# Gate rows made in four column strips of the array and spread to all partitions by DMA through device memory

## The chip, the cores and the metric

The kernel runs on one core of a Trainium2 chip. The core has a matrix engine (TensorE, called PE in the profile, with its weight loads as PEld), a vector engine (VectorE, DVE), a scalar engine (ScalarE, ACT), a general engine (GpSimd, POOL) and a synchronisation engine (SyncE, SP). Each runs its own instructions strictly in order and waits on semaphores for the others. The metric is the device time of one execution in microseconds; lower is better. Before the change the median of three runs is 1042.11 us (1041.72 to 1042.24).

## The reference, cut to what matters

Two transformer layers run over x of shape (4, 1024, 256), in float32. The first layer modulates its three branches by nine vectors made from a condition vector per batch entry; three of the nine are gates that multiply what a branch adds to x:

```python
m = silu(mod) @ w_ada + b_ada                      # (4, 9*256)
sh_msa, sc_msa, g_msa, sh_mca, sc_mca, g_mca, sh_mlp, sc_mlp, g_mlp = split(m, 9)
x = x + self_attn(ln(x) * (1 + sc_msa) + sh_msa) * g_msa       # ends in  o @ w_so + b_so
x = x + topk_cross_attn(ln(x) * (1 + sc_mca) + sh_mca) * g_mca # ends in  o @ w_co + b_co
x = x + swiglu(ln(x) * (1 + sc_mlp) + sh_mlp) * g_mlp          # ends in  h @ w_m2 + b_m2
```

The second layer is a cross-attention without gates. Self-attention works in windows of 128 tokens, and the cross-attention of the first layer keeps the 16 largest scores of 77 for each head and token.

## The kernel before

The 4 x 1024 tokens are cut into 16 units of 256 tokens, four to a batch entry b. Each unit passes five stages: windowed self-attention, selection of the top 16 scores, the cross-attention with them, the MLP, and the attention of the second layer. All units are written down as operations of a planner (`Plan`, lines 222 to 379): an operation has an engine, a cost, a function that issues its instructions, the buffers that it reads and writes, and a priority. `place` puts the operations in an order by these costs and priorities, and `issue` calls the functions in the order of their planned starts. So the order of instructions on each engine is fixed when the program is built, and the planned costs set it, not the measured ones. Where the plan has a gap on PE, `issue` fills it with small matmuls (line 1335) on a bank that is free.

A gate multiplies a whole output row, so the kernel multiplies it into the weight columns and the bias row instead: w_so, w_co and w_m2 (and b_so, b_co, b_m2) are loaded anew for each b and multiplied on POOL by the gate of that b. This takes two steps.

First, once, in `mod_gate(i)` (lines 721 to 731) for each of the three gates: PE multiplies the four silu'd condition vectors, held as columns in `sc_t`, by a chunk of w_ada (line 727), which gives 4 rows of 256 in a bank of the accumulator memory (PSUM), and DVE adds the bias row and stores them in `gates`, 4 partitions of 3 x 256 (line 730). `sc_t` is padded with zeros to 32 columns. The neighbour `mod_group` (line 699) works differently: it splits its chunk into four parts of 128 columns, and each part is multiplied in its own strip of 32 columns of the array, so that part j lands on partitions 32j to 32j+31.

Second, in `gated(b)` (lines 1292 to 1314), twelve times (b = 0 to 3, three gates): the row of b must stand on all 128 partitions. PE does this with a matmul whose stationary operand is one column of the identity, broadcast to 128 columns (line 1303); ACT copies the result from the bank to an SBUF buffer `gate` (line 1306; there are two such buffers); and POOL multiplies first the bias row (line 1308) and then the weights (line 1310) by it. The multiply of the weights waits for their load, and the load for the last reader of the buffer's old contents, so it can come much later than that of the row.

Other lines that the text below speaks of: 592, every load of weights, rows and biases, issued from SP (but for two bias loads at the start, which ACT issues); 699 and 706, strips and transpose of the other modulations; 748 and 755, transposes and modulation of the second layer's context; 767, 771, 780 and 783, keys and values of the context; 902, 905, 907, 909 and 912, a layer norm: statistics on DVE, the power -1/2 on POOL, subtract and multiply on DVE; 919, its transpose on PE; 926, the modulation on ACT; 938 and 1075, projections; 961 to 973, the shift that makes exponentials safe (POOL, PE, ACT); 985 and 996, scores and their maxima; 1098 and 1104, scores again with the shift, into the one buffer `s`; 1108, the exponential; 1116, times the values; 1008 to 1025, the division by the sum (ACT, POOL, DVE); 1035 and 1044, the output projection and its addition to x; 1049, the addition of the gated bias row to x on POOL; 1145 to 1166, the top-16 selection on DVE; 1247 and 1275, the MLP.

Of the kernel before, what the change touches and what calls it, by code (L numbers as in the profile page):

```python
# [9 lines left out]
F32 = mybir.dt.float32  # L10
BF16 = mybir.dt.bfloat16
AF = mybir.ActivationFunctionType
ALU = mybir.AluOpType
# [3 lines left out]
P = 128  # L17
# [371 lines left out]
def tile_block(ctx: ExitStack, tc: tile.TileContext, a: dict, out: bass.AP):  # L389
    nc = tc.nc  # L390

    x_d, cond_d, ctx_d = a["x"], a["cond_1024"], a["ctx_1024"]
    B, L, C = x_d.shape
# [3 lines left out]
    KC = C // P  # L397
# [12 lines left out]
    def ctile(shape, name, dt=F32):  # L410
        return const.tile(shape, dt, tag=name, name=name)
# [7 lines left out]
    ident = ctile([P, P], "ident")  # L419
# [25 lines left out]
    for i in range(3):  # L445
        t = ctile([P, TU, 4, 32], f"parts{i}", BF16)
# [5 lines left out]
    for i in range(2):  # L452
        t = ctile([P, TU, H // 2, VP], f"v_self{i}")
# [3 lines left out]
    pl = Plan()  # L457


    def f_pe(cols, n):  # L460
        return n * (cols * 0.00175 + 0.0095) + 0.1

    def f_act(n):
        return 0.21 + 0.00081 * n

    def f_dve(n):
        return 0.155 + 0.00104 * n

    def f_pool(n):
        return 0.13 + 0.00222 * n  # L470
# [7 lines left out]
    T_GATE = ("D", "D", 0.22, 0.05, 0.37, 0.216)  # L478
# [7 lines left out]
    def f_dma(kb):  # L486
        return max(0.4, kb / 260.0)


    def fixed(name, shape, dt=F32):  # L490
        return pl.fixed(ctile(shape, name, dt), name)
# [7 lines left out]
    bp = fixed("bp", [P, C])  # L499
    n_mod = 26  # L500
    mod = fixed("mod", [P, n_mod, B])
    gates = fixed("gates", [B, 3, C])
    k_ctx = [fixed(f"k_{i}", [P, KC, B, 2, LC]) for i in range(2)]
    v_ctx = [fixed(f"v_{i}", [LC, B, H // 2, VP]) for i in range(2)]
    for v, fill in zip(v_ctx, (0.0, 1.0)):
# [7 lines left out]
    start, total = {}, 0  # L513
# [6 lines left out]
    class Place:  # L520
# [21 lines left out]
        def buf(self, name, shape):  # L542
            ap, lo = self.ap(shape)
            b = pl.fixed(ap, name)
            early.append((lo, self.at, b))
            return b
# [12 lines left out]
    at = Place(0)  # L559
# [3 lines left out]

    sc_t = at.buf("sc_t", [P, KC, 32])
    nc.gpsimd.memset(sc_t(), 0.0)
    bg_ada = at.buf("bg_ada", [B, 3, C])
    cx = at.buf("cx", [LC, B, C])
    cn = at.buf("cn", [LC, B, C])
    w_kv = [at.buf("w_kv0", [P, KC, 2 * C])]
# [3 lines left out]
    at = Place(start["slab"])  # L573
# [15 lines left out]
    def load(buf, src, kb, prio, key=None, eng="SP", view=None):  # L589
        def fn():  # L590
            dst = buf() if view is None else view(buf())
            (nc.sync if eng == "SP" else nc.scalar).dma_start(dst, src)
        pl.op(eng, f_dma(kb) if eng == "SP" else 0.3, fn, w=[buf if key is None else (buf, key)],
              prio=prio, lag=2.0)
# [8 lines left out]
    def row_bc(buf, name, lo, prio, key=None, view=None, np_=P):  # L603
        load(buf, a[name][lo : lo + C].partition_broadcast(np_), np_, prio, key, view=view)
# [11 lines left out]
    for g, names in enumerate(groups):  # L616
        for name, hi in names:
            n, r = hi // P, n_rows[g]
# [2 lines left out]
            col_of[name] = (g, r)  # L621
            n_rows[g] += n
    for i in range(3):
        row_bc(bg_ada, "L0_xcond_b_ada", (3 * i + 2) * C, (-79.5, -59.5, -49.5)[i], i, lambda t, i=i: t[:, i, :], B)
    row_bc(bv_self, "L0_xcond_b_qkv", 2 * C, -81)
    row_bc(bv_ctx[0], "L0_xcond_b_kv", C, -66)
    row_bc(bv_ctx[1], "L1_xcond_bkv", C, -29.5)
# [2 lines left out]
    def chunk(name, lo, n, prio):  # L630
        c = pl.buf("chunk", f"{name}{lo}")
        load(c, a[name].rearrange("(kc p) n -> p kc n", p=P)[:, :, lo : lo + n], n, prio,
             view=lambda t: t[:, :, :n])
        early.append((chunk_lo, chunk_hi, c))
        return c
# [85 lines left out]
    def mod_gate(i, prio, dma_prio):  # L721
        c = chunk("L0_xcond_w_ada", (3 * i + 2) * C, C, dma_prio)
        pp = pl.buf("mm", f"modg{i}")

        def fn():
            for kc in range(KC):
                nc.tensor.matmul(pp()[:B, :C], sc_t()[:, kc, :B], c()[:, kc, :C],
                                 start=(kc == 0), stop=(kc == KC - 1))
        pl.op("PE", f_pe(C, 2), fn, w=[pp], r=[sc_t, c], prio=prio)
        pl.op("DVE", f_dve(256), lambda: nc.vector.tensor_tensor(  # L730
            gates()[:, i, :], pp()[:B, :C], bg_ada()[:, i, :], ALU.add), w=[(gates, i)], r=[pp, (bg_ada, i)], prio=prio)

    def filled(v):

# [55 lines left out]
    for i, key in enumerate("kqv"):  # L790
        weight(w_qkv, "L0_xcond_w_qkv", -84 + i, (1, 0, 2)[i] * C, C, key)
    mod_gate(0, -30, -79)
    mod_group("L0_xcond_w_ada", 3 * C, 6, False, -3, -70)
    load(cx, ctx_d.rearrange("b k c -> k b c"), 308, -69)
    weight(w_kv[0], "L0_xcond_w_kv", -68)
    weight(w_q0, "L0_xcond_w_q", -67)
    mod_gate(1, -2, -59)
    mod_group("L0_xcond_w_ada", 6 * C, 12, False, -1, -50)
    mod_gate(2, -1, -49)
    mod_group("L1_xcond_Wss_q", 0, 18, True, -1, -48)  # L800
    mod_group("L1_xcond_Wss_kv", 0, 22, True, -1, -47)
    for q in range(4):
        lo = (q % 2) * HID + (q // 2) * 4 * P
# [7 lines left out]
    for b in range(B):  # L811
        pl.op("DVE", 0.42, lambda b=b: nc.vector.bn_stats(st_c()[:LC, b, :], cx()[:, b, :]),
              w=[(st_c, b)], r=[cx], prio=-1)
    for b in range(B):
        pl.op("DVE", 0.16, lambda b=b: nc.vector.bn_aggr(mv_c()[:LC, b, :], st_c()[:LC, b, :]),
              w=[(mv_c, b)], r=[(st_c, b)], prio=-1)
# [475 lines left out]
    def gated(b, pr):  # L1292

        gw = {}
        for i, (key, name, kc) in enumerate(
            (("so", "L0_xcond_w_so", KC), ("co", "L0_xcond_w_co", KC), ("m2", "L0_xcond_w_m2", NF))
        ):
            first = None if b else DMA_FIRST[i]
            w, row = pl.buf("w_" + key, f"w_{key}{b}"), pl.buf("row", f"b_{key}{b}")
            gate, pg = pl.buf("gate", f"gate{b}{i}"), pl.buf("mm", f"pg{b}{i}")  # L1300
            load(w, a[name].rearrange("(kc p) n -> p kc n", p=P), 128 * kc, first or pr)
            load(row, a[f"L0_xcond_b_{key}"].partition_broadcast(P), 128, first or pr)
            pl.op("PE:gate", T_GATE, lambda i=i, pg=pg: nc.tensor.matmul(
                pg()[:, :C], ident[:B, b : b + 1].to_broadcast([B, P]), gates()[:, i, :], start=True, stop=True),
                w=[pg], r=[(gates, i)], prio=pr, take=[gate])
            pl.op("ACT:gate", f_act(256), lambda gate=gate, pg=pg: nc.scalar.copy(gate(), pg()[:, :C]),
                  w=[gate], r=[pg], prio=pr)
            pl.op("POOL:gate", f_pool(256), lambda row=row, gate=gate: nc.gpsimd.tensor_tensor(
                row(), row(), gate(), ALU.mult), w=[row], r=[row, gate], prio=pr)
            pl.op("POOL:gate", f_pool(256 * kc), lambda w=w, gate=gate, kc=kc: nc.gpsimd.tensor_tensor(  # L1310
                w(), w(), gate().unsqueeze(1).to_broadcast([P, kc, C]), ALU.mult),
                w=[w], r=[w, gate], prio=pr)
            gw["b_" + key], gw["w_" + key] = row, w
        return gw

    stages = (self_attention, selection, cross_attention, mlp, last_attention)
    for b in range(B):
        pl.at = None
        gw = gated(b, b * NU - 0.5)
        for part in range(NU):  # L1320
            u = Unit()
            u.b, u.part, u.name = b, part, f"_{b}{part}"
            u.prio = float(b * NU + part)
            pl.at = None
            u.x = pl.buf("x", "x" + u.name)
            move_x(u, x_d, False)
            for k, stage in enumerate(stages):
                pl.at = (b * NU + part, k)
                u.prio = ORDER[b * NU + part][k]
                stage(u, gw)  # L1330
# [45 lines left out]
```

## Time and profile before

| what | value |
|---|---|
| median of 3 runs | 1042.11 us |
| the profiled execution, its own time | 1041.43 us |
| its span, first to last instruction | 1039.4 us |
| mean granted TensorE clock | 0.993 |
| DVE, ACT and POOL busy | 73%, 70%, 52% of the span |
| line 1303, spread of the gates: PE | 24 records, 9.6 us busy |
| line 1306, copy of the gates: ACT | 12 instructions, 386 ns in the mean |
| line 1308, row times gate: POOL | 12 instructions, 724 ns; 33.9 us idle before them |
| line 1310, weights times gate: POOL | 12 instructions, 1.27 us for 512 columns, 4.53 us for 2048 |
| line 727, making the gates: PE | 12 records, 3.1 us busy |
| line 730, bias of the gates: DVE | 3 instructions, 412 ns |

A line of a timeline holds the start in us, the busy time in us, the engine, the line of the kernel, the operation, what it writes and reads with shapes, how many instructions of that kind were merged, and in brackets how long the engine was idle before it and what released it. One float32 matmul shows as two records. A granted clock of 1.00 is TensorE's full speed.

### The profile page before, as it was taken

The numbers are of one execution on the slowest core, as the hardware profiler recorded it, in microseconds if no ns is written. First come the engines' busy times: TensorE is split into PE (matmuls) and PEld (weight loads), VectorE is DVE, ScalarE is ACT, GpSimd is POOL, SyncE is SP. The second block draws the span as 40 slices with busy tenths as digits, with TensorE's granted clock in tenths as the row PEclk, the third lists the DMA queues.
The fourth block names the chain that finished last, engine by engine and source line by source line (L and its number), as shares of the span: only waits on it lengthen the run. The fifth ranks groups of instructions, "written<-read, shape, count | busy, mean of one in ns | idle before, by whom it ended". The sixth has DMA issues, their size and how long they took to land.

```text
span 1039.4 us, 27476 instructions
## 1 busy us (share of the span) xinstructions
PE 1012.0 (97%) x10363; PEld 770.5 (74%) x10363; DVE 757.3 (73%) x4000; ACT 723.5 (70%) x1270; POOL 542.1 (52%) x751
## 2 busy tenths in 40 slices
PE   7899999999999999999999999999999999999997
PEld 5667777777777778777877777778767787778775
DVE  5177999979899999947833446599999977724232
ACT  3358786687687794758468667877688765764665
POOL 3384445466353573557635647546335464753653
PEclk9799999999999999999999999999999999999999
DMA  7710000001000000100000200000000001000000
GB/s 255 242 50 7 3 2 1 3 3 36 3 22 27 7 3 5 38 16 22 21 1 2 82 22 21 2 2 2 2 2 22 2 2 42 12 1 12 2 21 21
DMA packets 23623, 27.01 MB, mean 26 GB/s; under 512 B 1609, under 2 KB 20675, under 8 KB 23491
## 3 DMA queue, kind: packets, MB, share of 16 engines
q1 hardware_dynamic: 23455, 25.26, 7.7%
q8 instruction: 81, 1.33, 0.5%
q14 instruction: 52, 0.42, 0.1%
q10 hardware_dynamic: 35, 0.01, 0.0%
HBM read 21.07 MB, written 4.19 MB: 24 GB/s over the span
## 4 chain that ended last, share of the span: by engine, by line
PE 48%; DVE 13%; ACT 6%; POOL 2%; issue 1%; POOLq 0%; ACTq 0%; DVEq 0%
PE mm L1247 13%; PE mm L1275 8%; PE mm L938 5%; PE mm L1035 5%; PE s L1196 4%; PE o L1212 3%; PE s L985 3%; DVE share L1153 2%; DVE r L1147 2%; DVE nm L996 2%; PE s L1186 1%; DVE share L1145 1%; DVE share L1151 1%; PE mm L919 1%; ACT prob L1108 1%
## 5 line engine op out<-in xcount | busy, mean ns | idle before, releaser
L1247 PE MATMUL mm<-share,w_m 128*128 128x256 f32 x640 | 150.3, 386 | 0.4 <-ACT share L926 0.2
L1205 ACT ACTIVATE prob<-s 77x2048 f32<-77x2048 f32 x64 | 120.0, 1875 | 43.7 <-PE s L1201 43.4
L996 DVE TENSOR_REDUCE nm<-s 128x16 f32<-128x2048 f32 (+1 forms) x64 | 119.0, 1859 | 38.0 <-PE s L985 17.2
L1247 PEld LDWEIGHTS mm<-share,w_m 128*128 128x128 f32 x640 | 117.7, 190 | 26.0 <-issue 4.7
L1147 DVE MATCH_REPLACE8 r<-share 128x77 f32<-128x77 f32 x512 | 109.9, 222 | 0.0
L1145 DVE MAX8 share<-share 128x8 f32<-128x77 f32 x512 | 94.4, 225 | 21.0 <-ACT share L1138 21.0
L1153 DVE MATCH_REPLACE8 share<-share,r 128x77 f32<-128x77 f32 x512 | 109.6, 221 | 0.0
L1011 POOL TENSOR_TENSOR share<-share 128x256 f32<-128x256 f32 x64 | 47.1, 736 | 96.4 <-ACT share L1008 95.1
L1151 DVE MAX8 share<-r 128x8 f32<-128x77 f32 x512 | 93.9, 224 | 0.0
L1247 PE MATMUL mm<-slab,w_m 128*128 128x256 f32 x384 | 92.9, 388 | 0.7 <-ACT slab L926 0.5
L1023 POOL TENSOR_TENSOR slab<-slab,share 128x256 f32<-128x256 f32 x96 | 69.4, 730 | 28.4 <-ACT share L1018 19.2
L1261 POOL TENSOR_SCALAR slab<-slab 128x512 f32<-128x512 f32 x43 | 64.4, 1498 | 36.8 <-ACT slab L1259 33.0
L1247 PEld LDWEIGHTS mm<-slab,w_m 128*128 128x128 f32 x384 | 69.9, 190 | 15.6 <-issue 3.1
L1275 PE MATMUL mm<-share,slab 128*128 128x256 f32 x344 | 80.9, 381 | 0.0
L1008 ACT ACTIVATE share<-o,mask 128x256 f32<-128x256 f32 x128 | 66.6, 575 | 12.2 <-PE o L1212 9.6
L1108 ACT ACTIVATE prob<-s 128x2048 f32<-128x2048 f32 x32 | 60.5, 1889 | 17.9 <-PE s L1104 17.5
L1044 DVE TENSOR_TENSOR slab<-slab,mm 128x512 f32<-128x512 f32 x52 | 35.4, 680 | 50.9 <-PE mm L1035 25.7
L1275 PEld LDWEIGHTS mm<-share,slab 128*128 128x128 f32 x344 | 64.7, 190 | 10.0 <-issue 0.9
L1253 ACT ACTIVATE slab<-mm,cols 128x256 f32<-128x256 f32 x90 | 43.0, 480 | 41.0 <-PE mm L1247 40.5
L1212 PE MATMUL o<-prob,v 77*32 77x256 f32 x1024 | 67.9, 385 | 0.8 <-ACT share L1018 0.5
L1049 POOL TENSOR_TENSOR slab<-slab,row 128x512 f32<-128x512 f32 x39 | 49.9, 1278 | 28.5 <-DVE slab L912 15.4
L907 POOL TENSOR_SCALAR rs<-mv 128x2 f32<-128x2 f32 x64 | 14.2, 222 | 81.7 <-DVE mv L905 78.8
(183 smaller groups left out, 2427.0 us busy)
## 6 DMA issues: line engine op xcount, KB each, us to landing
share<-in_L_xcond_w_m_dram SPq DMA_DIRECT2D x4, 1024.0 KB
slab<-in_x_dram SPq DMA_DIRECT2D x9, 256.0 KB, 2.9
out_dram<-slab SPq DMA_DIRECT2D x9, 256.0 KB, 2.7
w_m<-in_L_xcond_w_m_dram SPq DMA_DIRECT2D x4, 512.0 KB, 6.8
share<-in_L_xcond_w_ada_dram SPq DMA_DIRECT2D x3, 512.0 KB, 3.8
w_so<-in_L_xcond_w_so_dram SPq DMA_DIRECT2D x4, 256.0 KB
w_co<-in_L_xcond_w_co_dram SPq DMA_DIRECT2D x4, 256.0 KB, 4.0
w_qkv<-in_L_xcond_w_qkv_dram SPq DMA_DIRECT2D x3, 256.0 KB
```

What stands on the lines that cost most here:

```text
L996: pl.op("DVE:max", f_dve(n), lambda: nc.vector.tensor_reduce(nm()[:, t], s4(), AX.X, ALU.max, negate=True), w=[(nm, t)], r=[s], prio=u.prio)
L1008: pl.op("ACT:nln", 0.5, lambda e=e, own=own, other=other: nc.scalar.activation(nz()[:, e, :], o()[:, ts(e, UT)], AF.Ln, bias=own, scale=ot ...
L1023: nc.gpsimd.tensor_tensor(dst, dst, shaped(nz()[:, k, :], dst), op)
L1108: pl.op("ACT:exp", f_act(2048), lambda s=s, prob=prob: nc.scalar.activation(prob(), s(), AF.Exp), w=[prob], r=[s], prio=pr)
L1145: nc.vector.max(top()[:, h + i, 0:8], sc()[:, h + i])
L1147: nc.vector.match_replace(r1()[:, i], top()[:, h + i, 0:8], sc()[:, h + i], NEG)
L1151: nc.vector.max(top()[:, h + i, 8:16], r1()[:, i])
L1153: nc.vector.match_replace(sc()[:, h + i], top()[:, h + i, 8:16], r1()[:, i], NEG)
L1205: pl.op("ACT:exp", f_act(2048), lambda s=s, prob=prob: nc.scalar.activation(prob()[:LC], s()[:LC], AF.Exp), w=[prob], r=[s], prio=pr)
L1212: nc.tensor.matmul(o()[r, :UT] if drops is not None else o()[r, ts(e, UT)], columns(v_z()[:, b], 8 * c + 2 * j + e), prob()[:LC, j, ts(e, ...
L1247: nc.tensor.matmul(pp()[:, ts(half, UT)], w_m1()[:, kc, m : m + P], ht()[:, kc, :], start=(kc == 0), stop=(kc == KC - 1))
L1275: nc.tensor.matmul(pp()[:, ts(t, C)], gts[f // 2]()[:, f % 2, ts(t, P)], w_m2()[:, f, :], start=(f == 0), stop=(f == NF - 1))
```

## The change

The gates are made in four strips of the array, as the other modulations are: for each half of the contraction four matmuls of 64 columns take the place of one of 256. The row of gate i and batch entry b then lies in four pieces of 64 numbers on partitions b, 32+b, 64+b and 96+b. DVE's addition works on 128 partitions of 64, and the bias that it adds is loaded as 128 runs of 64 numbers instead of 4 of 256. Right after that addition POOL issues a DMA that writes the 128 x 64 block to device memory. In `gated`, the operation of PE issues no matmul any more: it issues, on POOL's queue, a DMA that reads the four pieces back from device memory into all 128 partitions of `gate`. ACT's copy issues nothing. Both operations stay in the plan with their old engines and costs, so the planned order is the same; only what they issue differs. The kernel before issues no DMA from POOL at all; the changed one issues three writes of 32 KB and twelve reads of 128 KB there.

```diff
-    gates = fixed("gates", [B, 3, C])
+    gates = fixed("gates", [P, 3, C // 4])
+    dram = ctx.enter_context(tc.tile_pool(name="dram", bufs=1, space=bass.MemoryType.DRAM))
+    gates_d = [dram.tile([P, C // 4], F32, tag=f"gates_d{i}", name=f"gates_d{i}") for i in range(3)]
...
-    bg_ada = at.buf("bg_ada", [B, 3, C])
+    bg_ada = at.buf("bg_ada", [P, 3, C // 4])
...
     for i in range(3):
-        row_bc(bg_ada, "L0_xcond_b_ada", (3 * i + 2) * C, (-79.5, -59.5, -49.5)[i], i, lambda t, i=i: t[:, i, :], B)
+        lo = (3 * i + 2) * C
+        load(bg_ada, a["L0_xcond_b_ada"][lo : lo + C].rearrange("(j o n) -> j o n", j=4, o=1).to_broadcast([4, 32, C // 4]),
+             B, (-79.5, -59.5, -49.5)[i], i, view=lambda t, i=i: t[:, i, :])
...
             for kc in range(KC):
-                nc.tensor.matmul(pp()[:B, :C], sc_t()[:, kc, :B], c()[:, kc, :C],
-                                 start=(kc == 0), stop=(kc == KC - 1))
+                for j in range(4):
+                    nc.tensor.matmul(pp()[32 * j : 32 * j + 32, : C // 4], sc_t()[:, kc, :], c()[:, kc, ts(j, C // 4)],
+                                     start=(kc == 0), stop=(kc == KC - 1))
         pl.op("PE", f_pe(C, 2), fn, w=[pp], r=[sc_t, c], prio=prio)
-        pl.op("DVE", f_dve(256), lambda: nc.vector.tensor_tensor(
-            gates()[:, i, :], pp()[:B, :C], bg_ada()[:, i, :], ALU.add), w=[(gates, i)], r=[pp, (bg_ada, i)], prio=prio)
+        def add():
+            nc.vector.tensor_tensor(gates()[:, i, :], pp()[:, : C // 4], bg_ada()[:, i, :], ALU.add)
+            nc.gpsimd.dma_start(gates_d[i], gates()[:, i, :])
+        pl.op("DVE", f_dve(256), add, w=[(gates, i)], r=[pp, (bg_ada, i)], prio=prio)
...
-            pl.op("PE:gate", T_GATE, lambda i=i, pg=pg: nc.tensor.matmul(
-                pg()[:, :C], ident[:B, b : b + 1].to_broadcast([B, P]), gates()[:, i, :], start=True, stop=True),
+            pl.op("PE:gate", T_GATE, lambda i=i, gate=gate: nc.gpsimd.dma_start(
+                gate().rearrange("p (j n) -> p j n", j=4),
+                gates_d[i].rearrange("(j r) n -> r j n", j=4)[b].partition_broadcast(P)),
                 w=[pg], r=[(gates, i)], prio=pr, take=[gate])
-            pl.op("ACT:gate", f_act(256), lambda gate=gate, pg=pg: nc.scalar.copy(gate(), pg()[:, :C]),
-                  w=[gate], r=[pg], prio=pr)
+            pl.op("ACT:gate", f_act(256), lambda: None, w=[gate], r=[pg], prio=pr)
```

## The prediction

> **What bounds the kernel.** I read the page's busy shares and slices first:
>
> ```profile
> PE 1012.0 (97%) x10363; PEld 770.5 (74%) x10363; DVE 757.3 (73%) x4000; ACT 723.5 (70%) x1270; POOL 542.1 (52%) x751
> ...
> DVE  5177999979899999947833446599999977724232
> ...
> PEclk9799999999999999999999999999999999999999
> DMA  7710000001000000100000200000000001000000
> ```
>
> PE is full, but DVE is nearly full in slices 4 to 16 (104 to 442 us, with dips at 7 and 8), and slice 1 (26 to 52 us) has DMA traffic and a low clock; by windows of 1 us it is 0.50 from 36 to 48 us. The chain of waits could be followed back only to 309.8 us; of those 730 us PE has 68%, DVE 19%.
>
> Next, who waits for the spreading matmuls (the view of line 1303; idle columns are us, times):
>
> ```profile
> L1303 PE MATMUL mm<-gates,ident x24: 372/454/791, 34.5 to 563.7; 4*128 4x256 f32 x24
> ...
> who waited for it (us, times):
>   ACT gate L1306: 7.4, 4
> ```
>
> Then POOL's timeline, since all new work lands on its queue:
>
> ```profile
> 35.63 0.72 POOL L1308 TENSOR_TENSOR row<-row,gate 128x256 f32<-128x256 f32 x1 [11.50 <-DMA w_m<-in_L_xcond_w_m_dram]
> 36.32 1.26 POOL L1310 TENSOR_TENSOR w_so<-w_so,gate 128x512 f32<-128x512 f32 x1
> 38.98 0.72 POOL L1308 TENSOR_TENSOR row<-row,gate 128x256 f32<-128x256 f32 x1 [1.41 <-ACT gate L1306]
> 39.66 1.27 POOL L1310 TENSOR_TENSOR w_co<-w_co,gate 128x512 f32<-128x512 f32 x1
> ...
> 46.80 0.72 POOL L1308 TENSOR_TENSOR row<-row,gate 128x256 f32<-128x256 f32 x1
> 52.09 0.73 POOL L1011 TENSOR_TENSOR share<-share 128x256 f32<-128x256 f32 x1 [4.56 <-ACT share L1008]
> ```
>
> The first batch of gates ends at 47.5 and leaves POOL 4.56 us of slack. Later gates have less:
>
> ```profile
> 118.71 0.73 POOL L1308 TENSOR_TENSOR row<-row,gate 128x256 f32<-128x256 f32 x1 [2.59 <-ACT gate L1306]
> 119.40 1.28 POOL L1049 TENSOR_TENSOR slab<-slab,row 128x512 f32<-128x512 f32 x1
> 120.76 0.22 POOL L907 TENSOR_SCALAR rs<-mv 128x2 f32<-128x2 f32 x1
> 121.07 0.71 POOL L909 TENSOR_TENSOR rs<-rs,mhalf 128x2 f32<-128x2 f32 x1
> ```
>
> That rs, done at 121.78, is used by DVE's L912 at 121.91, with DVE full: 0.13 us of slack.
>
> **What goes.** Twelve spreading matmuls at about 0.62 us a pair (0.59 to 0.69 in PE's timeline where nothing is interleaved): 7.4 us of PE. Worth on the path: at 527.88 the pair is on the chain, -0.6. At 89.93 PE is full (19.95 of 20 us between 80 and 100), -0.6. At 103.66, 117.53, 336.08 and 507.29 DVE is full or the chain, at 271.32 filler follows, at 563.40 the chain is on ACT: 0. The four between 34 and 43 us run at half clock; without them the second L1098 (46.91) could start 1.6 us sooner, but the division it leads to (POOL L1011) is behind POOL, see below: 0. Twelve ACT copies of 0.37: none on the chain, 0. Making the gates: line 699 does 512 columns in strips in 0.65 us, so 256 take at least 0.33, against 0.96 now; at most -0.6 three times, but PE waits at 33.12 for a load anyway: 0. DVE's addition of 64 columns: 0.2 shorter, 0. The bias loads of 128 runs cost SP 0.47 instead of 0.28 (the row of bv_self): +0.2, under SP's later wait of 8.9 us for PE; without that cover +0.6. Sum: **-1.2**.
>
> **What comes.** No DMA issued by POOL is in this trace. Each read is 512 runs of 256 B. Holding POOL: at least 0.4 (SP issues a row load in 0.34 to 0.47 us). POOL's own slope is (4.53-1.27)/1536 = 2.1 ns an element; one such step a run is 0.2+1.1 = 1.3 us, two (read and write side in turn) 2.4. I take 1.3. Then landing: quiet, x loads of 256 KB take 2.9 us from issue; 128 KB row loads, nearest in size and broadcast, all took longer:
>
> ```profile
> DMA to landing us min/median/max: 4.6/5.6/6.7
> ```
>
> Less SP's issue of 0.4 that is 2.5 quiet and 5.2 beside the weight loads (DMA share about 0.9 from 31 to 50 us). So a read lands 3.8 us after its start when quiet, 6.5 early.
>
> *Early batch.* Queue order on POOL: write of gate 2 (after DVE at 31.2, done 31.7), read 0, row, w_so, read 1, read 2 (same buffer as read 0, so behind w_so), row, w_co, L1049, a read for b=1, w_m2, row, L1011. Read 0 starts at 31.7, lands 38.2; row and w_so to 40.2; reads 1 and 2 hold POOL to 42.8; read 1 lands 46.7; row, w_co, L1049 to 49.9; the next read to 51.2; w_m2 (4.5) and row to 56.5. L1011 is **4.4 us late** (52.09). Behind it stand the rs at 52.90, then DVE L912 (54.91) and PE's transpose at 56.04. POOL's gap of 1.44 before 55.36 takes up part; after it there is none until 66.9 us, and DVE's L912 at 63.50 waits for that queue: **+3.0**.
>
> *Gate 0 of b=2.* Read issued at 116.12, lands 119.9, not 118.71: 1.2 late, less 0.13: **+1.1** on a full DVE.
>
> *The rest.* Issued ahead into idle stretches of 6.26, 4.14 and 8.49 us that now end at ACT's copy or a maximum (107.77, 272.54, 530.88): hidden; with no stretch each would cost 1.3. At 94.67 read at 91.7, 0.8 late, taken by the gap of 1.78 before 100.09. At 337.25 1.8 late, but PE needs the parts at 341.67, 1.6 after they were made, and 0.96 of gap lies between. At 508.37 2.2 late, gap of 4.02 behind it. At 573.49 the read starts eight multiplies ahead. All 0.
>
> Sum: -1.2+3.0+1.1 = **+2.9**: 1041.43 becomes 1044.3; runs had a median 0.7 above that execution, so **1045.0**.
>
> **Rules weighed.** The Trainium skill (DMA: Bandwidth & Descriptors, Anatomy of one DMA) gives 2.0 us plus bytes/436e3 for a DMA from POOL: an estimate of 2.3 us for 128 KB, against my row's 5.2. With it a read lands 3.6 after issue, the early batch ends at 50.6, before 52.09, and the sum is -1.2+0.9 = -0.3: 1041.8. I stay with the row: same size, same broadcast, same stretch. Against the change speaks SBUF — State Buffer, SBUF: two separate sides: POOL cannot write descriptors while DVE holds the port both share, 0.62 us becoming 3.1 in its example. The trace shows such sharing: L912 twice at 508.90 takes 1.69 us beside POOL's L1310, 0.72 at 121.91. By the rule the read at 116.12 would be 2.5 later, sum +5.4; but the DVE work beside it then is a maximum (L996), of another kind, so I add nothing and keep this for the range.
>
> **Rivals.**
> 1. *Faster.* PE bounds all of it and POOL's waits are hidden: POOL loses 22.4 us of waiting for ACT's copies. 7.4 us times PE's share of 68% is -5.0: **1037**. It decides if reads land within 3.6 us and the early batch ends by 52. Against it: DVE is near full from 104 to 442 us.
> 2. *No change.* The rule's 2.3 us holds, gains and the late b=2 gate cancel: **1041.8**.
> 3. *Much slower.* POOL is held 2.4 us a read and reads land at the worst row's 6.3 behind that. The early batch then ends at 62.3, 10.2 late, +8.8; b=2 +2.2; at 337 +0.4; less 1.2: +10.2, **1052**. It decides if one read holds POOL over 2 us. Less work on PE in 28 to 43 us could also keep it at half clock longer, in the same direction.
>
> **Numbers.** Forecast 0.52 (own range 1043 to 1048), rival 1 0.17, rival 2 0.16, rival 3 0.15. A difference under 0.2% (2.1 us) is not told from none: of the forecast 0.10 falls inside. Faster 0.17; same 0.16+0.10 = 0.26; slower 0.42+0.15 = 0.57. The range 1038.5 to 1052 leaves out the better half of rival 1 and the worse half of rival 3.
>
> **What would show it.** In the changed profile: POOL's L1011 for unit 0 near 56 instead of 52 (rival 3: over 60; rivals 1 and 2: at 52 or before); POOL's issue of a read near 1.3 us; DVE idle about 1 us before L912 near 122; clock windows of 0.50 still ending near 48; POOL waiting for its own reads in place of ACT. I am wrong if POOL catches up before 52 us, or if the early lateness, visible at 60 us, is gone by 104 us where DVE fills.

## The result, and the profile after

| | before | after |
|---|---|---|
| time, median (range) | 1041.91 us (1041.71 to 1042.24, 4 runs) | 1071.16 us (1070.21 to 1073.40, 4 runs) |
| ratio | | 1.0283, 95% interval 1.0266 to 1.0301 |
| the profiled execution, its span | 1041.43, 1039.4 us | 1070.21, 1068.4 us |

The changed kernel is slower by 29 us. The sign was forecast, the size was not: +2.9 was expected, and the range ended at 1052.

The busy times of the changed kernel and its DMA row (40 slices of the span):

```profile
PE 1010.2 (95%) x10375; PEld 770.8 (72%) x10375; DVE 756.3 (71%) x4000; ACT 720.8 (67%) x1258; POOL 553.8 (52%) x766
...
DMA  7951300000100200100120311000000001000000
```

Every engine has nearly the same work as before, so 29 us are waiting. The DMA row shows where to look first: slices 1 to 3 are 9, 5 and 1 in place of 7, 1 and 0. The part on DMA queues has a column for the share of 16 engines' time:

```profile
q1 hardware_dynamic: 23827, 25.34, 7.7%
q0 software_dynamic: 672, 1.67, 4.5%
```

Queue 0 holds the writes and reads of the gates. It moves 1.67 MB and takes more than half as much engine time as the 25.34 MB of all other loads and stores. The view of the reads' line, with durations in ns and landing in us, and then of POOL's wait:

```profile
L1314 POOL DMA_DIRECT2D gate<-gates_d x12: 747/841/866, 30.7 to 592.1; - x12
...
who waited for it (us, times):
  POOL row L1319: 50.6, 8
...
DMA to landing us min/median/max: 4.9/8.3/13.5
```

One read holds POOL for 0.84 us, less than the 1.3 assumed. It lands after 8.3 us in the median; 3.8 (quiet) and 6.5 (early) were assumed.

**Where the time comes from.** DVE runs the same 4000 instructions in the same order in both kernels, so the start of each can be compared with that of its counterpart. The difference, called the shift below, is a staircase: -0.2 us at 20 us of the old time, up and down from 30 to 55 (between -4 and +12), about +10 from 56 to 100, +11 to 119, +19 from 127, +18 at 330, +25 from 351, +29 from 521, and it stays there to the end. So four places make the loss: one near 50 us (10 us) and three later ones (8, 7 and 3.4 us). The later ones look alike in POOL's timeline, where brackets hold the idle time and what ended it. At the first:

```profile
126.97 0.84 POOL L1314 DMA_DIRECT2D gate<-gates_d  x1
135.49 0.71 POOL L1319 TENSOR_TENSOR row<-row,gate 128x256 f32<-128x256 f32 x1 [7.68 <-DMA gate<-gates_d]
136.17 1.25 POOL L1059 TENSOR_TENSOR slab<-slab,row 128x512 f32<-128x512 f32 x1
137.51 0.22 POOL L917 TENSOR_SCALAR rs<-mv 128x2 f32<-128x2 f32 x1
137.81 0.73 POOL L919 TENSOR_TENSOR rs<-rs,mhalf 128x2 f32<-128x2 f32 x1
```

and DVE's timeline beside it:

```profile
138.57 0.73 DVE L922 TENSOR_SCALAR share<-slab,mv,rs 128x256 f32<-128x256 f32 x2 [5.63 <-POOL rs L919]
```

POOL stands 7.68 us for its own read. Behind that read are an addition and the rs that DVE needs: DVE, full in this stretch before, idles 5.63 us. The read issued at 353.67 lands at 362.03, with the parts for TensorE behind it; the one issued at 532.20 lands at 540.51.

The early place looks different. A window of 6 us, first in the kernel before, then in the changed one; behind the window and its length stand busy us and counts of PE, PEld, DVE, ACT and POOL, the granted clock, the DMA share (of 16 engines) and GB/s:

```profile
48.00:54.00 6.00, 6.00 (x111) 4.49 (x108) 1.80 (x8) 4.78 (x8) 1.67 (x3) 0.94 0.81 211
48.00:54.00 6.00, 6.00 (x48) 3.84 (x46) 0.00 (x0) 4.03 (x9) 3.47 (x4) 0.72 1.22 43
```

From 48 to 54 us the DMA engines show a share of 1.22 and move 43 GB/s; before the change it was 0.81 and 211 GB/s. (The view counts the whole time of a packet in the window where the packet starts, so a share can pass 1.) The queues of this window in the changed kernel, with packets, MB and share:

```profile
q0 software_dynamic: 54, 0.16, 114.6%
q1 hardware_dynamic: 104, 0.10, 7.3%
```

So nearly all of that time belongs to the gates' reads, and hardly anything else moves. SP's own timeline shows who suffers; the kernel before, then the changed one, for the five x loads of that stage (from the start of the first to the end of the last, SP's waits for earlier loads between them included):

```profile
39.60 6.53 SPq L892 DMA_DIRECT2D slab<-in_x_dram  x5
```

```profile
42.90 12.05 SPq L902 DMA_DIRECT2D slab<-in_x_dram  x5
```

Both POOL and DVE then start late:

```profile
57.55 4.50 POOL L1321 TENSOR_TENSOR share<-share,gate 128x2048 f32<-128x2048 f32 x1 [3.11 <-issue]
59.73 0.75 DVE L912 BATCH_NORM_STATS2 st<-slab 128x6 f32<-128x256 f32 x2 [15.44 <-DMA slab<-in_x_dram]
```

The view names no releaser for POOL, but the third read, issued at 43.89, lands after 13.5 us, at 57.4. So at 50 us there are two candidates, POOL's wait for the reads and the loads held up behind them, and the page alone does not tell which one counts. The clock is not a third: in the changed kernel it is 0.50 again from 60 to 68 us, but the shift does not grow over that stretch (11.6 us for the DVE instruction at 59.73, 10.9 for the one at 70.87).

### The profile page after: what moved, and what is told of

Read it like the earlier page. It is cut to its first block, busy times and chain, and to the rows that moved or that the text cites. A ratio compares the mean times of both kernels' runs of the same rounds, so it can differ in the third digit from the quotient of the medians.

```text
span 1068.4 us, 27505 instructions
## 1 busy us (share of the span) xinstructions
PE 1010.2 (95%) x10375; PEld 770.8 (72%) x10375; DVE 756.3 (71%) x4000; ACT 720.8 (67%) x1258; POOL 553.8 (52%) x766
## 3 DMA queue, kind: packets, MB, share of 16 engines
q1 hardware_dynamic: 23827, 25.34, 7.7%
q0 software_dynamic: 672, 1.67, 4.5%
## 4 chain that ended last, share of the span: by engine, by line
PE 60%; DVE 17%; ACT 8%; POOL 5%; DMA 4%; issue 3%; POOLq 0%; ACTq 0%; DVEq 0%
PE mm L1257 15%; PE mm L1285 8%; PE mm L948 7%; PE mm L1045 6%; PE s L995 5%; PE s L1206 5%; PE o L1222 4%; DVE r L1157 3%; DVE share L1163 3%; DVE nm L1006 2%; PE s L1196 2%; DVE share L1155 2%; DVE share L1161 2%; PE mm L929 2%; PE s L1108 2%
## 5 line engine op out<-in xcount | busy, mean ns | idle before, releaser
L1215 ACT ACTIVATE prob<-s 77x2048 f32<-77x2048 f32 x64 | 120.0, 1875 | 46.1 <-PE s L1211 45.7
L1006 DVE TENSOR_REDUCE nm<-s 128x16 f32<-128x2048 f32 (+1 forms) x64 | 119.0, 1859 | 39.8 <-PE s L995 19.3
L1021 POOL TENSOR_TENSOR share<-share 128x256 f32<-128x256 f32 x64 | 46.9, 732 | 87.7 <-ACT share L1018 83.2
L1118 ACT ACTIVATE prob<-s 128x2048 f32<-128x2048 f32 x32 | 60.3, 1885 | 16.7 <-PE s L1114 16.3
```

The lines of the kernel that those rows point to most:

```text
L1006: pl.op("DVE:max", f_dve(n), lambda: nc.vector.tensor_reduce(nm()[:, t], s4(), AX.X, ALU.max, negate=True), w=[(nm, t)], r=[s], prio=u.prio)
L1215: pl.op("ACT:exp", f_act(2048), lambda s=s, prob=prob: nc.scalar.activation(prob()[:LC], s()[:LC], AF.Exp), w=[prob], r=[s], prio=pr)
```

## The experiments

The theory after this reading, W: the reads land late, and POOL, which takes its queue in order, holds up what stands behind them. Three questions followed. Do the strips cost anything? Is it the wait or the traffic? Why does a read of 128 KB take 8 us?

The expectations speak of a step "at 111 us". Taken instruction by instruction, that step lies at the read issued at 126.97 shown above; the read issued at 111.23 costs 1 us. Ratios below are against the kernel before on the same chip, whose median was 1039.8 to 1041.9.

**Strips without the DRAM trip.**

```diff
-            pl.op("PE:gate", ... nc.gpsimd.dma_start(gate(), ... gates_d[i] ...)
+                for j in range(4):
+                    nc.tensor.matmul(pg()[:, ts(j, C // 4)], ident[:, 32 * j + b : 32 * j + b + 1].to_broadcast([P, P]),
+                                     gates()[:, i, :], start=True, stop=True)
...
-            pl.op("ACT:gate", f_act(256), lambda: None, w=[gate], r=[pg], prio=pr)
+            pl.op("ACT:gate", f_act(256), lambda gate=gate, pg=pg: nc.scalar.copy(gate(), pg()[:, :C]), ...)
```

> Strips kept in all three gate products, but the gates are carried by TensorE again (four 64-column products with a column of the identity, into the same PSUM buffer, and ScalarE's copy); no DRAM tile. Theory W (the loss is POOL waiting in its queue for reads that land 8 us late, strips cost nothing): 1040.5 to 1042.5, no wait of POOL for gates in the trace. Rival S (the strips or the reordered TensorE work around them cost part of it): over 1045, and the shift against the kernel before starts at the strips near 28 us.

(The DRAM tiles and the writes go too.) Measured 1045.46 us, ratio 1.0038 (1.0018 to 1.0057). No wait of POOL for a gate from DRAM is left, and of the shift of 29 us only 3.7, in five steps of 0.5 to 0.9 us. The time is 3 us above the upper end of theory W and just inside the range of rival S, but the shift does not begin at 28 us: it is 0.7 from 50 to 100. This kernel cannot say whether the rest comes from the strips or from its own spread, which takes 96 TensorE records where the kernel before had 24. The runs with strips and a fast read, below, have a shift of 0.2 to 0.5 us from 70 to 100 us and 1.3 at the end, so the strips cost no more than that.

**Only batch 0 by TensorE.** The same edit for `b == 0` alone; the nine later reads and all writes stay.

```diff
+            pl.op("PE:gate", T_GATE, read if b else spread, w=[pg], r=[(gates, i)], prio=pr, take=[gate])
```

> As the changed kernel, but the three gates of batch 0 are carried by TensorE and only the nine of batches 1 to 3 are read from DRAM (the three writes stay). Theory W: the 10 us of the first 100 us go and the later three steps (8.0, 7.4, 3.4 us) stay, so about 1061 (1058 to 1063). Rival C (the later steps come from the order in which the late first batch left the engines): the later steps shrink too, 1042 to 1052. Rival T (the early writes, not the reads, disturb the loads): over 1065.

Measured 1061.87 us, ratio 1.0199 (1.0183 to 1.0214). The shift is -0.1 at 50 to 100 us, then 8.1, 16.8 and 20.3: the early step is gone, and the later three have about the size they had (1.3 us of the second comes earlier, near 292). They do not come from the early lateness, so the two parts add up.

**Reads issued long before they are needed.** Four gate buffers, and each read from the fifth on issued tens of us before it is needed, at fixed places.

```diff
-    ring("gate", 2, [P, C])
+    gbc = [pool.tile([P, C], F32, tag=f"gbc{i}", name=f"gbc{i}") for i in range(4)]
+    ahead = []
...
+                if (b, i) == (1, 0):
+                    ahead.append(lambda: [read(k, 1) for k in (1, 2)])
+                if i == 2 and 1 <= b < B - 1:
+                    ahead.append(lambda: [read(k, b + 1) for k in range(3)])
```

> As the changed kernel (same reads, same bytes, same queue), with four gate buffers in place of two; reads 5 to 12 are issued tens of us before they are needed: the second and third of batch 1 after its first weight product, those of batches 2 and 3 after the last weight product of the batch before. The first four are where they were. Theory W: the steps at 111, 353 and 532 us go, the early 10 us stay: 1051 to 1054, later waits for gates under 1 us in all. Rival D (what costs is the traffic of the reads, wherever it is put: 512 runs of 256 B in the path of the other transfers): 1062 or more, with idle time behind x and weight loads near the new places.

Measured 1054.26 us, ratio 1.0133 (1.0116 to 1.0150). In this kernel the products of batch 2 use what the buffers hold and not their own gates, so it could not show their wait. A second kernel therefore has the reads in the order of use, every product waiting for its own gate; `queue` holds the reads still to be issued, and `flush` issues them as soon as one of the four buffers is free:

```diff
+            if (n, i) == (1, 0):
+                queue.extend((k // 3, k % 3) for k in range(4, 3 * B))
+            flush()
```

> As the changed kernel (strips 8 KB apart, POOL's queue), with four gate buffers; from the second read of batch 1 on, each read is issued as soon as a buffer is free, in the order of use, and every product uses its own gate. Theory W: the steps at 111, 353 and 532 us go and the early 10 us stay: 1052 to 1055. Rival D (the traffic itself costs, wherever it is put): 1060 or more.

Measured 1054.19 us, ratio 1.0133 (1.0112 to 1.0154): shift 14.0 after the early stage, 12.4 at the end, and no step upwards between. The same slow reads, issued early enough, cost nothing at the later places. There the loss is the wait. (Why the early stage costs 11.1 us in the first of these kernels and 14.0 in the second, in place of 9.9, stays open.)

**The early traffic with nobody waiting for it.** Batch 0's three reads go into buffers that nothing uses.

```diff
+                nc.gpsimd.dma_start((gate() if b else unused[i]()).rearrange("p (j n) -> p j n", j=4), ...)
+                if b == 0:
+                    spread(i, pg)
```

> As the changed kernel, but for batch 0 the three reads from DRAM go into three buffers that nothing uses, at the same places of POOL's queue, and TensorE carries the gates; batches 1 to 3 are as in the changed kernel. It splits the early 10 us. Theory P (POOL's wait for the reads makes them): they go, as without the reads at all, and 1060 to 1063 remain. Rival L (the slow reads keep the DMA engines from the weight and x loads of that stage): most of the 10 us stays, 1066 to 1072, with the load of w_m still landing near 46 us.

Measured 1072.19 us, ratio 1.0309 (1.0290 to 1.0327): rival L. POOL's and SP's timelines of this kernel:

```profile
41.15 1.26 POOL L1331 TENSOR_TENSOR w_co<-w_co,gate 128x512 f32<-128x512 f32 x1
...
53.78 4.50 POOL L1331 TENSOR_TENSOR share<-share,gate 128x2048 f32<-128x2048 f32 x1 [9.41 <-DMA share<-in_L_xcond_Wkv_dram]
```

```profile
42.04 17.91 SPq L903 DMA_DIRECT2D slab<-in_x_dram  x5
```

The first two gates are through by 42.4 us, where the changed kernel needed until 52.5, and still the shift is 10.5 us. POOL stands 9.41 us before the product of the 1024 KB weights. The view names another load, Wkv, but it is the load of these weights themselves that lands then. The chain of waits has it from issue to landing, in the changed kernel and in this one:

```profile
33.41 12.31 DMA share<-in_L_xcond_w_m_dram
```

```profile
33.41 20.20 DMA share<-in_L_xcond_w_m_dram
```

It landed at 45.7 us there and at 53.6 here. So one part of the expectation, w_m still landing near 46 us, did not hold: since POOL does not wait, the second and third read leave at 38.45 us in place of 43.09 and fall on this load, and the x loads behind it come later still. The run shows that the traffic of the three reads is enough to lose the 10 us, with no wait of POOL for them. It is not the changed kernel with the wait alone taken out; what the wait would cost without the traffic was not run.

**The queue.** The reads are issued from ScalarE's queue.

```diff
-            pl.op("ACT:gate", f_act(256), lambda: None, w=[gate], r=[pg], prio=pr)
+            pl.op("ACT:gate", f_act(256), lambda i=i, gate=gate: nc.scalar.dma_start(gate() ..., gates_d[i] ...), ...)
```

> As the changed kernel, with the twelve reads issued from ScalarE's queue, at the place of the old copy, in place of POOL's; the three writes stay on POOL. Theory N (the 512 runs of 256 B set the landing, whatever queue issues them): landing stays at 7 to 9 us, POOL still waits 40 to 55 us for gates, and only POOL's 0.8 us of hold per read goes: 1062 to 1072. Rival Q (POOL's own queue is what makes them slow): landing 3 to 4.5 us, as the row loads have on the other queue, time 1042 to 1050.

Measured 1083.05 us, ratio 1.0398 (1.0383 to 1.0414). The trace gives the landing of one of these reads alone, the one issued at 117.02, and it is 7.7 us; POOL still waits 56.7 us for gates, in nine places. So POOL's queue is not what makes the reads slow. It is worse than the changed kernel at least in part because a read now waits for its turn behind ScalarE's work: two of them were issued at 117.02 and 135.43 us in place of 111.23 and 126.97.

**Length, number and place of the pieces.** First, gates made as before the change and rows of 1 KB in DRAM:

```diff
+    gates_d = [dram.tile([B, C], F32, tag=f"gates_d{i}", name=f"gates_d{i}") for i in range(3)]
...
+            nc.gpsimd.dma_start(gates_d[i], gates()[:, i, :])
...
+                gate(), gates_d[i][b].partition_broadcast(P)),
```

> The gates are made as before the change (four partitions of 256 columns), written as four rows of 1 KB and read by POOL's queue at the same places as in the changed kernel, 128 runs of 1 KB in place of 512 of 256 B. Theory R (the number of short runs sets the landing): landing falls from 8.3 us to 4 to 5 us, waits of POOL for gates from 51 us to under 20, time 1045 to 1055. Rival H (all partitions reading the same few addresses sets it, whatever the run): landing stays near 8 us and the time at 1065 to 1072.

Measured 1046.63 us, ratio 1.0060 (1.0042 to 1.0079), landing 3.3 us. That spoke for R, the number of runs. The next two kernels keep 512 runs of 256 B and move only their addresses. In the first the reads of batches 1 to 3 take other data, 512 pieces of x, in place of the gates:

```diff
+            src = x_d[b][: 4 * P].rearrange("(p j) (q n) -> q p j n", j=4, q=4)[i] if b else (...)
```

> As the changed kernel, but the nine reads of batches 1 to 3 take 512 runs of 256 B at 512 different addresses of the input x, in place of four addresses for all partitions (their values are not the gates); batch 0 is unchanged. Theory N (the number of short runs sets it): transfers stay at 3.2 to 6.7 us, steps at 111, 353 and 532 us stay, 1065 to 1072. Rival H (all partitions reading the same few addresses sets it): transfers fall to 1.5 to 2 us, about the 1.6 us that the reads in rows of 1 KB took, the later steps shrink to under 2 us each, 1052 to 1058.

Measured 1052.62 us, ratio 1.0104 (1.0089 to 1.0120); these nine reads land in 2.8 us (median). In the second the four pieces of a row lie side by side:

```diff
-    gates_d = [dram.tile([P, C // 4], F32, ...
+    gates_d = [dram.tile([32, C], F32, ...
...
-            nc.gpsimd.dma_start(gates_d[i], gates()[:, i, :])
+            nc.gpsimd.dma_start(gates_d[i].rearrange("r (j n) -> j r n", j=4), gates()[:, i, :])
...
-    ring("gate", 2, [P, C])
+    ring("gate", 2, [P, 4, C // 4 + 1])
...
```

> Strips, order and queue as in the changed kernel, but a batch's four pieces lie side by side in DRAM, in one row of 1 KB; the gate's buffer has a gap of 4 B after each piece, so that a read is still 512 runs of 256 B. Theory N (number of runs): landing stays near 8 us, 1063 to 1073. Rival A (the four pieces 8 KB apart are what is slow): landing 3 to 4.5 us as with rows of 1 KB, 1045 to 1050. The products of POOL may take a little longer for the gap.

Measured 1043.82 us, ratio 1.0021 (1.0009 to 1.0032). Its queue and the view of its reads:

```profile
q0 software_dynamic: 720, 1.68, 0.8%
```

```profile
L1314 POOL DMA_DIRECT2D gate<-gates_d x12: 754/843/866, 30.6 to 564.4; - x12
...
DMA to landing us min/median/max: 3.5/3.8/6.4
```

Theory N falls, and with it R: 512 pieces of 256 B on the same queue at the same places, with the same hold of POOL, land in 3.8 us, and 27 of the 29 us are gone. What was left was the 8 KB between the pieces: in the changed kernel all 128 partitions read the same four addresses, each 8 KB from the next. Four more kernels change the pitch, the distance from one piece to the next. In the first and third only the width of the tile differs (2112 = 33 x 64 and 4096 = 64 x 64 numbers a strip), in the second a batch's pieces are rows of one tile, in the fourth the source is x again. The cuts are of the first, the second and the fourth; the writes go to the same places as the reads:

```diff
+    gates_d = [dram.tile([4, 2112], F32, tag=f"gates_d{i}", name=f"gates_d{i}") for i in range(3)]
...
+                gates_d[i][:, : 32 * (C // 4)].rearrange("j (r n) -> r j n", n=C // 4)[b].partition_broadcast(P)),
```

```diff
+                gates_d[i].rearrange("(r j) n -> r j n", j=4)[b, :, : C // 4].partition_broadcast(P)),
```

```diff
+            src = x_d.rearrange("b l c -> (b l) c").rearrange(
+                "(p j k) (q n) -> k q p j n", j=4, k=8, q=4)[2 * b - 1, i] if b else (...)
```

> As the changed kernel, with the four strips 8.25 KB apart in DRAM in place of 8 KB, nothing else. Theory B (a pitch of just 8 KB makes the four pieces fall on one another): transfers of 131 KB fall from 6.5 us to 1.6 to 2 us, time 1043 to 1048. Rival J (any four pieces lying far apart are slow when all partitions read them): transfers stay at 3.2 to 6.7 us, time 1065 to 1073.

> As the changed kernel, with a batch's four pieces 1 KB apart in DRAM. Theories B and J both: fast, 1.6 to 2 us a transfer and 1043 to 1048; only a theory in which the pieces must touch (so that they count as one row of 1 KB) has it slow, at 3 us or more a transfer and over 1055.

> As the changed kernel, with the four strips 16 KB apart in DRAM in place of 8 KB. If any multiple of 8 KB makes the pieces fall on one another: transfers of 3.2 to 6.7 us and 1065 to 1073. If only 8 KB itself does: 1.6 to 2 us and 1044 to 1048.

> As the changed kernel, but the nine reads of batches 1 to 3 take 512 pieces of 256 B from the input x at 512 different addresses, each 8 KB from the next (their values are not the gates). Theory B: an 8 KB pitch is slow even when no address is read twice, 3.2 us a transfer or more, 1060 to 1075. Rival H2 (it takes both, few addresses far apart and all partitions reading them): fast, 0.8 to 2 us a transfer, about 1052 as with the 512 close addresses.

| pieces of a read | addresses | landing, median us | time, us |
|---|---|---|---|
| side by side (256 B) | 4, shared | 3.8 | 1043.8 |
| 1 KB apart | 4, shared | 3.6 | 1044.5 |
| 8 KB apart (the change) | 4, shared | 8.3 | 1071.2 |
| 8.25 KB apart | 4, shared | 3.9 | 1046.2 |
| 16 KB apart | 4, shared | 8.1 | 1071.6 |
| 1 KB apart, in x (b = 1 to 3) | 512, own | 2.8 | 1052.6 |
| 8 KB apart, in x (b = 1 to 3) | 512, own | 2.7 | 1053.5 |

(In the last two rows the three reads of batch 0 are still the shared ones 8 KB apart, so the early 10 us are in their time. The kernels with 8.25 and 16 KB, 1 KB shared and 8 KB own were run once each.) It takes both: few addresses that all partitions read, and a pitch of 8 or 16 KB. Neither alone is slow, with the reserve that the reads with own addresses take another tensor, x. Adding 256 B to the pitch is enough. Gate 1's reads were faster than the others (131 KB in 3.2 us against 6.2 to 6.7, from first to last packet), and a further kernel asks whether that goes with the address:

```diff
-    gates_d = [... for i in range(3)]
+    gates_d = [... for i in (1, 0, 2)]
+    gates_d = [gates_d[i] for i in (1, 0, 2)]
```

> As the changed kernel, with the DRAM tiles of gates 0 and 1 laid out in the other order. In the changed kernel gate 1's reads moved in 3.2 us, those of gates 0 and 2 in 6.2 to 6.7. If the speed goes with the address, gate 0 is fast now (3.2 us) and gate 1 slow; if with the place in the program, nothing changes. Time: the first step of the later ones (at 111 us) is gate 2's or gate 0's read, so 1062 to 1072 in either case.

Measured 1069.89 us, in one run. With the tiles declared in the other order nothing changed: the read of gate 1 was again the fast one (3.1 us). Where the tiles end up in device memory was not looked at, so this stays open.

**A version meant to keep the gain.** Packed rows, each read as one run of 1 KB, and the nine later reads from SP's queue:

```diff
+                nc.sync.dma_start(row(), a[f"L0_xcond_b_{key}"].partition_broadcast(P))
+                if b:
+                    queue.append((b, i))
+                    flush()
```

> A version meant to keep what the strips may give: strips, a batch's row packed to 1 KB in DRAM, batch 0 read by POOL's queue as in the changed kernel, the nine later reads issued from SP's queue behind the load of the same row, into four gate buffers, long before they are used. If the packed read and the wait for it were all that was left, the later shifts vanish and the first one of about 0.6 us stays: 1041.5 to 1043 (within 0.2% of before). If SP, waiting for a gate buffer, holds up the loads of x behind it, 1045 or more with DVE waiting for x.

Measured 1042.81 us, ratio 1.0019 (1.0011 to 1.0027). The shift is +0.2 from 70 to 290 us, at most +2.1 behind that and +1.3 at the end. No version here beats the kernel before. This one is 0.2% slower with no wait left for later gates, so what the strips and twelve matmuls fewer may bring is less than what the packed reads still cost.

## Why the prediction was off, by its steps

- **Strips and removed matmuls, -1.2.** Not contradicted, not shown. With strips and reads far ahead the shift at the end was +1.3, so whatever PE gains there is smaller than what the reads still cost.
- **POOL's hold of 1.3 us a read.** 0.84 us: too dear, within its bounds of 0.4 to 2.4.
- **Landing 3.8 us quiet.** The term that failed: 8.3 us. Its nearest rows were broadcast loads of 128 KB, but those read one address range of 1 KB; no row of the trace read four shared addresses 8 KB apart. With pieces side by side the landing was 3.8 us, the number assumed, and that kernel was 1.9 us slower than the kernel before, where +2.9 was forecast. The nearness of these two totals is in part luck: its shift after the early stage was 0.5 (+3.0 forecast), it rose by 0.9 at gate 0 of b=2 (+1.1) and by 1.0 at the read of 337.25 (0).
- **Gate 0 of b=2, +1.1.** The right place: the read issued at 126.97. By the same sum a landing 4.7 us longer (8.5 for 3.8) makes it +5.8; the shift rose there from 11.0 to 16.7 us at the first L922 behind it. At 126 us of the old time it rose to 18.8: DVE's maximum (L1006) stands 2.06 us for PE's scores, for which the sum has no term.
- **The rest, 0.** The reads at 337.25 and 508.37, priced as hidden, cost 7 and 3.4 us. At 508.37 the slack was real and too small for the longer landing: 2.2 + 4.5 - 4.02 = 2.7, near the measured 3.4. At 337.25 the slack was misread. Its 1.6 us are the time from the first group of parts (made at 340.07) to PE's use of the second at 341.67, and the second was made at 341.16. The nearest user is DVE, which takes the rs behind the parts at once; POOL and DVE before the change, then DVE after it:

```profile
341.56 0.72 POOL L909 TENSOR_TENSOR rs<-rs,mhalf 128x2 f32<-128x2 f32 x1
```

```profile
342.31 1.02 DVE L912 TENSOR_SCALAR slab<-slab,mv,rs 128x256 f32<-128x256 f32 x2
```

```profile
366.07 1.04 DVE L922 TENSOR_SCALAR slab<-slab,mv,rs 128x256 f32<-128x256 f32 x2 [5.74 <-POOL rs L919]
```

  The slack is 0.03 us. By it the forecast here should have been 1.8 - 0.96 - 0.03 = +0.8, and with 4.5 us more of landing 5.3, close to the 5.74 that DVE stands. At 107.77 the idle stretch took most of the lateness, 1 us came through.
- **Early batch, +3.0.** The wrong mechanism as well as the wrong size. It counted POOL's queue alone. POOL's L1021 was late, at 62.70 where 56 was forecast, but when POOL did not wait for the reads the stage was as late (10.5 us). The reads occupied the DMA engines that SP's weight and x loads needed in that stage, and that was priced only as a slower landing of the reads, never as slower loads. The sign of the clock did not come either: the stretch at 0.50 ended near 42 us, not 48.
- **The range.** Rival 3 reached to 8.7 us of early landing and 1052, but let the landing vary in the early stage alone, not at the later places, where the three later steps came from it.
- **Rules weighed.** The fit of the Trainium skill (DMA: Bandwidth & Descriptors, Anatomy of one DMA), an estimate of 2.3 us, makes 3.6 us from issue with the assumed hold, against the row's 3.8. Packed reads took 3.5 to 4.0 us at the quiet places, so there both were right, and up to 6.4 early, where the row's 6.5 was the better; neither has the 8.3 us of pieces 8 KB apart. The rule on the shared port is not needed to explain anything here: packed and strided reads held POOL the same 0.84 us.

## What to carry to other kernels

When a value is passed through device memory, price the layout of what is read back, not its bytes: look at which addresses all partitions share and how far apart they are, and pack what one reader takes side by side. A slow transfer has two prices, one for the engine that waits and one for every other load that needs the same DMA engines; a run with the transfer and without the wait, beside one with the transfer issued early, shows them apart. And where slack is to hide a step, look for the nearest user of what comes late on every engine, and vary the uncertain term until the slack stops hiding it: at 508.37 it would by its sum have held up to a landing of about 5.6 us, and not at 8.2.

## What the runs showed of the hardware

Four pieces of 256 B read by all 128 partitions are slow at a pitch of 8 or 16 KB (8.3 and 8.1 us to landing) and not at 1 KB or 8.25 KB (3.6 and 3.9), all from POOL's queue. At 8 KB they are slow from ScalarE's too (7.7). The Trainium skill (DMA: Bandwidth & Descriptors, Latency and other measured facts) reports the like for row pitches at large powers of two: a pitch of 4 MiB halves the rate of a copy, and a pad of 4 KiB heals it while one of 192 B does not. Here the pitch is far smaller, 256 B of pad are enough, and 512 own addresses at 8 KB are not slow (2.7 us), so that entry describes a relative, not the same case; that channels of the memory are what collide is an inference there, and no run here shows it. And a slow read is seen by its neighbours: five x loads took 12 to 18 us of SP's queue in place of 6.5, while in the 6 us from 48 on the DMA engines looked busier than before (share 1.22 in place of 0.81) and moved a fifth of the bytes (43 in place of 211 GB/s). A high DMA share with few GB/s is the sign to look for.
